# A graph attention layer on one core: edge values from four 64x64 products, weights in PSUM, clip on ScalarE, a new pace of the picks

## The chip, the core and the metric
One core of a Trainium2 chip. TensorE (PE; its weight loads are PEld) multiplies matrices into PSUM, VectorE (DVE) and ScalarE (ACT) work element by element on SBUF and PSUM, GpSimd (POOL) issues indirect DMAs, SyncE (SP) the plain ones. The metric is the time of one execution in microseconds on the device; lower is better.

## What is computed
6250 nodes with 64 features, 206250 edges sorted by destination, four heads of 16:

```python
score = (Kh[src] * Qh[dst] * (1.0 / np.sqrt(D)) * Ee).sum(-1)
score = jnp.exp(jnp.clip(score, -5.0, 5.0))
msg = Vh[src] * score[..., None]
wV = jax.ops.segment_sum(msg, dst, num_segments=n)
```
Kh, Qh and Vh are linear maps of the nodes' x, Ee is one of the edges' own 64 features (We, be). The output is layernorm(x + wV). All inputs are float32.

## The kernel before
Edges come in 1612 tiles of 128, in 202 groups of eight (g, the last one of four); two groups make a step s, except at the end. A first stage writes a table of K and V to memory and keeps a second form of x (parts, three bf16 parts) in SBUF. Then comes one loop over g, unrolled and written in the order in which each engine executes it: each engine works off its own instructions in that order, and waits for others by semaphores that the framework sets from the tiles that are read and written.

For each group:
- **K and V of the sources** (kv) come in two ways. Most tiles are fetched by one indirect DMA each, on POOL (gather_kv, L260), for a step four steps ahead. Two tiles in each of some groups are "picked" instead: DVE builds one-hot rows (hots, L644, pieces of up to five blocks, named hot), PE multiplies them with parts (picks, three products for each of 25 blocks of nodes), DVE selects the half (picked, L666), PE multiplies by the weights (picked_kv), ACT puts the result into kv (place_kv, L679). A batch is four tiles; 25 blocks are spread over three groups (9, 8 and 8) by first_unit, and 62 batches fit.
- **Edge values**: edges (L689) multiplies the block-diagonal 128x128 we_sb with the features of eight tiles, 128x512 in float32, into PSUM ee; two tiles lie above each other on the partitions. biased (L695, ACT) adds be and writes eb. It runs three groups ahead.
- **Queries**: queries multiplies one-hot rows (to, made on ACT at L243 and L249) with Q into qq, two halves of 64 partitions. terms (L708, DVE) multiplies eb by qq; turn (L713, PE) transposes the result into qe, one PSUM bank for even and one for odd g.
- **Scores**: products (L732 to L737, DVE) multiplies kv by qe, sums over each head and clips to -5 and 5; weigh (L741, ACT) is Exp; message (L753, DVE) multiplies V by the weights, both in SBUF, into qe.
- **Sum by destination**: keep (ACT, L765) and take (DVE, L770) split the message into three bf16 parts; sums (PE) multiplies them, once for each step, with one-hot columns of the destinations (of, L724, DVE) into pa, which shares a PSUM bank, room, with sum_. add (L805, L811, DVE) adds the three parts into sum_ and that into two rows of blocks, two groups after the step's end.

All products of the loop go through the helper product, so they have line 684; they are told apart by their tiles: pick, room (sums), ee, qq. Sums of a step are put between the picks of the next group, four after every two blocks, and the rest behind turn and queries. The add stands at the end of a group, except in the last steps.

PSUM is full: still (constants for the one-hots), room, two for picks, ee, qq, two of qe.

Of the kernel before, what the change touches and what calls it, by code (L numbers as in the profile page):

```python
# [1 line left out]

# [5 lines left out]
F32 = mybir.dt.float32  # L8
# [18 lines left out]
NS = len(STEPS)  # L27
NR2 = 112
ONES = NS - 8
# [18 lines left out]
TABLES = 4  # L48
BIG = N // P
REST = N - BIG * P  # L50


def tiles_of(g):
    return min(G, T - g * G)
# [6 lines left out]
def groups_of(s):  # L61
    return range(STEPS[s][0], STEPS[s][0] + STEPS[s][1])
# [5 lines left out]
UNITS = NB // 2  # L68
MOST = 5
LEAD = 6  # L70
# [2 lines left out]

def first_unit(g):

    return UNITS * ((g - LEAD) // 3) + (0, 9, 17)[(g - LEAD) % 3]


def when(k):
# [48 lines left out]
def tile_gnn(ctx: ExitStack, tc: tile.TileContext, x, x_blocks, by_rows, xT, wT, bias, beT, weT, eT, src, src_rows, dst,  # L128
             dst_rows, out):
    nc = tc.nc  # L130
    consts = ctx.enter_context(tc.tile_pool(name="consts", bufs=1))
# [28 lines left out]
    ident = consts.tile([P, P], F32, name="ident")  # L160
# [6 lines left out]
    row_b = consts.tile([P, 1], BF16, name="row_b")  # L167
    minus_row3 = consts.tile([P, 1], F32, name="minus_row3")
    one_p = consts.tile([P, 1], F32, name="one_p")
    ones_b = consts.tile([3, P], BF16, name="ones_b")  # L170
    key = consts.tile([P, T, 2], BF16, name="key")
    key_i = consts.tile([P, KEYS], I32, name="key_i")
# [6 lines left out]
    we_sb = consts.tile([P, 2 * C], F32, name="we_sb")  # L179
# [5 lines left out]
    be_col = consts.tile([P, 1], F32, name="be_col")  # L185
# [11 lines left out]
    ET, QW, at = {}, {}, {}  # L197
    SRC, FROM, ODD, KB, TO = ({} for _ in range(5))
# [89 lines left out]
    with tc.tile_pool(name="nodes", bufs=1) as nodes, \  # L288
# [27 lines left out]
        for i in range(NB // CB):  # L316
            s = slice(i * CB * P, (i + 1) * CB * P)
# [63 lines left out]
        def constants():  # L381
            nc.vector.tensor_scalar(from_row, row, -float(NB // 2), P + 0.75, op0=OP.mult, op1=OP.add)
            nc.vector.tensor_scalar(upper, row, C - 0.5, None, op0=OP.is_gt)
            nc.vector.tensor_copy(row_b, row_i)
            nc.vector.tensor_scalar(row_i, row_i, 1, None, op0=OP.arith_shift_right)
            nc.vector.tensor_scalar(half_b, row_i, P + 1.0, None, op0=OP.add)
            nc.vector.memset(one_p, 1.0)
            nc.vector.memset(ones_b, 1.0)

        def three_parts(out_, values, n, times):  # L390
# [206 lines left out]
    with tc.If(rv == 0) as branch:  # L597

        with tc.tile_pool(name="work", bufs=2) as work, \
                tc.tile_pool(name="accp", bufs=1) as accp, \  # L600
                tc.tile_pool(name="fixed", bufs=1, space=bass.MemoryType.PSUM) as fixed, \
                tc.tile_pool(name="psum", bufs=1, space=bass.MemoryType.PSUM) as psum:
            OH, OF, EB, TERM, MSG, SCORE, HOT = ({} for _ in range(7))
            still = fixed.tile([P, 4 * P], F32, name="still")
            col = still[:, :C].bitcast(BF16)
            block2 = still[:, C:C + NB].bitcast(BF16).rearrange("p (b c) -> p b c", c=2)
            nc.tensor.transpose(col, row_b[:, 0:1].to_broadcast([P, P]), ident_b)
            nc.tensor.transpose(still[:, C:C + NB].bitcast(BF16), half_b[:2 * NB].to_broadcast([2 * NB, P]),
                                ident_b[:2 * NB, :2 * NB])
            room = fixed.tile([P, 4 * P], F32, name="room")  # L610
            pa = room[:, :3 * C]
            sum_ = room[:, 3 * C:4 * C]
            px = [fixed.tile([P, 4 * P], F32, name=f"pick{k}") for k in range(2)]
            xs = [accp.tile([P, 4 * P], F32, name=f"x{k}") for k in range(2)]
            ee = fixed.tile([P, G // 2, P], F32, name="ee")
# [67 lines left out]
            def product(*aps, **kw):  # L683
                mark.append(nc.tensor.matmul(*aps, **kw))  # L684

            def edges(g):

                n = tiles_of(g) // 2
                product(ee[:, :n, :], we_sb, ET[g][:, :n, :], start=True, stop=True)  # L689

            def biased(g):

                n = tiles_of(g) // 2
                EB[g] = work.tile([P, G // 2, P], F32, name="eb")
                nc.scalar.activation(EB[g][:, :n], ee[:, :n], AF.Identity, bias=be_col)  # L695

            def queries(g):

                n = tiles_of(g)
                for u in range(2):  # L700
                    product(qq[u * C:(u + 1) * C, :n // 2, :], QW[g], TO[g][:, u:n:2, :],
                                     start=True, stop=True)

            def terms(g):
# [4 lines left out]

            def turn(g):  # L710

                for u in range(tiles_of(g) // 2):
                    nc.tensor.transpose(qe[g % 2][:, 2 * u:2 * u + 2, :].rearrange("p j c -> p (j c)"),  # L713
                                        TERM[g][:, u, :], ident)

            def onehot_edges(s):

# [11 lines left out]
            def products(g):  # L729
                n = tiles_of(g)  # L730
                prod = work.tile([P, G, C], F32, name="prod", bufs=1)
                nc.vector.tensor_mul(prod[:, :n, :], kv_of(g)[:, :n, :C], qe[g % 2][:, :n, :])  # L732
# [4 lines left out]
                nc.vector.tensor_scalar(score, score, -5.0, 5.0, op0=OP.max, op1=OP.min)  # L737

            def weigh(g):
                score = SCORE[g][:, :tiles_of(g)]  # L740
                nc.scalar.activation(score, score, AF.Exp)  # L741

            def message(g):
                s, k = place_of(g)
                n = tiles_of(g)
                if s < WHOLE:
                    if k == 0:
                        MSG[s] = work.tile([P, 2 * G, 3, C], BF16, name="msg")
                    to = qe[g % 2][:, :n, :]
                else:  # L750
                    MSG[s] = kvs[(s - 2) % KVB][:, G:, :C]
                    to = MSG[s][:, :n, :]
                nc.vector.tensor_mul(to.rearrange("p g (h d) -> p g h d", h=H),  # L753
                                     kv_of(g)[:, :n, C:].rearrange("p g (h d) -> p g h d", h=H),
                                     SCORE[g][:, :n, :, None].to_broadcast([P, n, H, D]))

            def part_of(g, i):

# [18 lines left out]

            def pa_of(s):

                return {NS - 3: px[0][:, :3 * C], NS - 2: px[1][:, :C], NS - 1: ee[:, 0, :C]}.get(s, pa)  # L780

            def sums(s, lo=0, hi=2 * G):
                n = tiles_in(s)
                for j in range(lo, min(hi, n)):
# [16 lines left out]
            def add(s):  # L801
                b = first_row(s) // P
                what = pa_of(s)
                if s < WHOLE:
                    nc.vector.tensor_reduce(sum_, what.rearrange("p (i c) -> p c i", i=3), axis=AX.X,  # L805
                                            op=OP.add)
                    what = sum_
                for k, mask in ((b, above), (b + 1, below)):
                    if 0 <= k < BIG + 1:
                        slot = slot_of(k)  # L810
                        nc.vector.scalar_tensor_tensor(slot, what, mask_of(mask, s), slot,  # L811
                                                       op0=OP.mult, op1=OP.add)
# [54 lines left out]
            for g in range(NG + 1):  # L867
# [36 lines left out]
                    hots(*mc)  # L904
                if parted:
                    take(g, 0)
                if g > groups_of(ONES - 1)[-1]:
                    for s in done:
                        add(s)
                if g - 1 in READY:  # L910
                    picked(READY.index(g - 1))
                if g - 2 in READY:
                    picked_kv(READY.index(g - 2))
                    place_kv(READY.index(g - 2))
                where.append(mark[-1])
# [231 lines left out]
```

## Time and profile before

| | us |
|---|---|
| median of 3 runs | 1745.33 (1743.85 to 1745.64) |
| the profiled execution | 1744.26 |
| its span, first to last instruction | 1742.4 |

The profile's page gives for each engine its busy time; groups of instructions by line with their tiles, count, busy time, mean duration in ns and the engine's idle time before them; the chain of waits, which goes back from the last instruction to whatever released it; and a timeline (start, duration, instruction). Each row of windows gives the length of a stretch and each engine's busy time in it. The time of one pass is read best as the distance between two starts, since matmuls are pipelined and a row's duration contains the pipeline's depth.

### The profile page before, as it was taken

Reading aid. Unit: us, or ns where it says so; the run is one execution under the profiler, and the core shown is the slowest. Engines: PE = TensorE matmul, PEld = TensorE weight load, DVE = VectorE, ACT = ScalarE, POOL = GpSimd, SP = SyncE. Lnnn points to the kernel's source line nnn. Section 1 sums busy time; section 2 is a strip of 40 time slices with the busy share of each in tenths; the row PEclk is TensorE's granted clock in tenths of the full one; section 3 lists DMA queues with packets and bytes.
Section 4 is the critical chain, followed back from the end, with each engine's and each line's share of the span. In section 5 each row is a group of like instructions: output and inputs, shape, how many; then the busy total and the mean of one; then the engine's idle time right before and its main releaser. Section 6 shows DMA issues by size and latency. Waiting matters only on the chain.

```text
span 1742.4 us, 26109 instructions
## 1 busy us (share of the span) xinstructions
PE 1661.7 (95%) x8456; PEld 881.2 (51%) x8611; DVE 1569.6 (90%) x2637; ACT 918.4 (53%) x1507; POOL 1310.5 (75%) x1374
## 2 busy tenths in 40 slices
PE   7779999999999999999999999999999999999964
PEld 6435555555555555555555555555555555555533
DVE  5689999999999999999999999999999999999976
ACT  3655555545555555555555555555555555555553
POOL 7777777777777777777777777777777777777775
PEclk9879999999999999999999999999999999999985
DMA  6744444343443443434434344344343443434331
GB/s 191 246 120 133 112 118 116 102 121 101 117 120 103 120 113 104 122 108 121 121 102 120 104 114 118 99 120 117 106 132 97 120 113 103 121 107 125 108 89 47
DMA packets 115144, 203.65 MB, mean 117 GB/s; under 512 B 55475, under 2 KB 56223, under 8 KB 114885
## 3 DMA queue, kind: packets, MB, share of 16 engines
q1 hardware_dynamic: 70914, 112.68, 21.7%
q0 software_dynamic: 43648, 88.17, 19.5%
q10 hardware_dynamic: 436, 1.04, 0.3%
q8 instruction: 69, 1.13, 0.3%
q14 instruction: 77, 0.63, 0.1%
HBM read 194.18 MB, written 7.59 MB: 116 GB/s over the span
## 4 chain that ended last, share of the span: by engine, by line
PE 90%; DMA 3%; DVE 2%; issue 2%; ACT 2%; POOL 1%; SPq 0%; POOLq 0%; DVEq 0%; ACTq 0%
PE pick L684 62%; PE ee L684 11%; PE room L684 7%; PE qe L713 5%; PE qq L684 4%; DMA kv<-kv_tab,src_i 2%; POOL kv L260 1%; PE ps L462 1%; DMA wkv<-in_wT 1%; DMA et<-in_eT 0%; PE pv L542 0%; DVE score L735 0%; DVE prod L732 0%; DVE term L708 0%; ACT eb L695 0%
## 5 line engine op out<-in xcount | busy, mean ns | idle before, releaser
L260 POOL DMA_INDIRECT kv<-kv_tab,src_i x1324 | 1270.7, 960 | 403.5 <-issue 197.1
L684 PE MATMUL pick<-hot,parts 128*128 128x512 bf16 x4495 | 1052.4, 379 | 8.3 <-issue 0.2
L684 PEld LDWEIGHTS <-parts 128*128 128x128 bf16 x4650 | 451.9, 98 | 527.1 <-issue 73.3
L644 DVE TENSOR_TENSOR hot<-from,still 128x2560 bf16<-128x2560 bf16 x366 | 460.0, 1257 | 0.0
L741 ACT ACTIVATE score<-score 128x32 f32<-128x32 f32 x202 | 46.3, 229 | 732.7 <-DVE score L737 732.7
L765 ACT ACTIVATE msg<-qe 128x512 bf16<-128x512 f32 x400 | 238.6, 596 | 35.8 <-DVE qe L753 26.9
L684 PE MATMUL ee<-et,we_sb 128*128 128x512 f32 x404 | 227.4, 645 | 7.1 <-ACT eb L695 6.1
L249 ACT ACTIVATE to<-to,one_p 126x1024 bf16<-126x1024 bf16 x198 | 226.5, 1144 | 0.0
L243 ACT ACTIVATE to<-kb,minus_row 126x1024 bf16<-126x1024 uint8 x198 | 224.6, 1134 | 0.0
L684 PE MATMUL room<-msg,of 128*128 128x192 bf16 x1592 | 200.2, 252 | 17.6 <-DVE y L811 11.3
L684 PEld LDWEIGHTS <-of 128*128 128x128 bf16 x1600 | 142.8, 100 | 109.5 <-DVE y L811 19.9
L770 DVE TENSOR_TENSOR msg<-qe,msg 128x512 bf16<-128x512 f32 x200 | 136.9, 685 | 67.4 <-ACT msg L765 61.3
L708 DVE TENSOR_TENSOR term<-eb,qq 128x512 f32<-128x512 f32 x202 | 137.0, 678 | 20.1 <-PE qq L684 15.8
L770 DVE TENSOR_TENSOR qe<-qe,msg 128x512 f32<-128x512 f32 x200 | 138.2, 691 | 18.2 <-ACT msg L765 18.2
L732 DVE TENSOR_TENSOR prod<-kv,qe 128x512 f32<-128x512 f32 x202 | 137.3, 680 | 8.2 <-DMA kv<-kv_tab,src_i 3.4
L735 DVE TENSOR_REDUCE score<-prod 128x32 f32<-128x512 f32 x202 | 138.3, 685 | 7.0
L713 PE MATMUL qe<-ident,term 128*128 128x128 f32 x806 | 126.2, 281 | 18.7 <-DVE term L708 18.7
L753 DVE TENSOR_TENSOR qe<-kv,score 128x512 f32<-128x512 f32 x200 | 139.0, 695 | 4.1 <-ACT score L741 4.1
L695 ACT ACTIVATE eb<-ee,be_col 128x512 f32<-128x512 f32 x202 | 135.1, 669 | 4.6 <-PE ee L684 4.6
L724 DVE TENSOR_TENSOR of<-still,key 128x2048 bf16<-128x2048 bf16 (+2 forms) x105 | 122.7, 1169 | 0.2
L713 PEld LDWEIGHTS qe<-ident,term 128*128 128x128 f32 x806 | 97.3, 144 | 49.8 <-DVE term L708 29.9
L684 PE MATMUL qq<-to,qw 126*64 126x512 bf16 x396 | 82.4, 413 | 0.0
(138 smaller groups left out, 855.5 us busy)
## 6 DMA issues: line engine op xcount, KB each, us to landing
et<-in_eT SPq DMA_DIRECT2D x100, 512.0 KB
kb<-key_tab SPq DMA_DIRECT2D x101, 252.0 KB
kv<-kv_tab,src_i POOLq DMA_INDIRECT x1324
srcs<-in_src_rows SPq DMA_DIRECT2D x62, 256.0 KB
qw<-q_tab SPq DMA_DIRECT2D x202, 15.8 KB
kv_tab<-kv_sb SPq DMA_DIRECT2D x4, 640.0 KB
q_tab<-q SPq DMA_DIRECT2D x5, 480.0 KB
y<-in_x_blocks SPq DMA_DIRECT2D x2, 512.0 KB
```

Of the source, the lines that this page charges most:

```text
L243: nc.scalar.activation(TO[g][:, :n, :], KB.pop(g)[:, :n * P].rearrange("p (j e) -> p j e", j=n), AF.Square, bias=minus_row3[:3 * W])
L249: nc.scalar.activation(TO[g][:, :n, :], TO[g][:, :n, :], AF.Relu, bias=one_p[:3 * W], scale=-1.0)
L260: return nc.gpsimd.indirect_dma_start(out=kv_of(g)[:, j, :], out_offset=None, in_=kv_tab[:, :], in_offset=bass.IndirectOffsetOnAxis(ap=src ...
L644: nc.vector.tensor_tensor(HOT[k][:, :hi - lo].rearrange("p b (a c) -> p b a c", c=2), pairs(FROM[m])[:, None].to_broadcast(shape), block2[ ...
L684: mark.append(nc.tensor.matmul(*aps, **kw))
L708: nc.vector.tensor_mul(TERM[g][:, :n], EB.pop(g)[:, :n], qq[:, :n])
L713: nc.tensor.transpose(qe[g % 2][:, 2 * u:2 * u + 2, :].rearrange("p j c -> p (j c)"), TERM[g][:, u, :], ident)
L732: nc.vector.tensor_mul(prod[:, :n, :], kv_of(g)[:, :n, :C], qe[g % 2][:, :n, :])
L735: nc.vector.tensor_reduce(score, prod[:, :n, :].rearrange("p g (h d) -> p g h d", h=H), axis=AX.X, op=OP.add)
L753: nc.vector.tensor_mul(to.rearrange("p g (h d) -> p g h d", h=H), kv_of(g)[:, :n, C:].rearrange("p g (h d) -> p g h d", h=H), SCORE[g][:, ...
L765: nc.scalar.activation(part, left, AF.Copy)
L770: nc.vector.tensor_sub(left if i == 0 else part_of(g, 2)[1], left, part)
```

## The change
- **Edge values** by four products for each group: weights and features are cut into two halves of 64 partitions (r), and each half into two halves of its tiles (u). Product (u, r) reads partitions of half r and writes partitions of half u. The two r go to two banks: room becomes two banks, and ee the first half of each. So tile k and tile k + 4 of a group now lie above each other, and queries, biased and turn follow.
- **Room**: pa and sum_ take the other half of the first bank; the other half of the second one holds three buffers of weights, and pa of the last step.
- **Weights** are written to PSUM by Exp. The clip leaves DVE: ACT makes Relu(5 - score), then Exp(5 - that), which is the exponential of the score's minimum with 5; the lower clip is the larger of the weight and exp(-5) inside the message's product, now a scalar_tensor_tensor.
- **Order**: sums stand behind queries as a whole; every add stands ahead of picked.
- **Picks**: 35 blocks in four groups instead of 25 in three. 65 batches fit, 12 more tiles are picked and as many fewer gathered.

```diff
-    return UNITS * ((g - LEAD) // 3) + (0, 9, 17)[(g - LEAD) % 3]
+    return (g - LEAD) * 35 // 4
...
-            room = fixed.tile([P, 4 * P], F32, name="room")
-            pa = room[:, :3 * C]
-            sum_ = room[:, 3 * C:4 * C]
+            room = fixed.tile([P, 2, 4 * P], F32, name="room")
+            ee = room[:, :, :2 * P].rearrange("p r (i e) -> p r i e", e=P)
+            pa = room[:, 0, 2 * P:2 * P + 3 * C]
+            sum_ = room[:, 0, 2 * P + 3 * C:2 * P + 4 * C]
+            weights = [room[:, 1, 2 * P + C + k * G * H:2 * P + C + (k + 1) * G * H]
+                       .rearrange("p (g h) -> p g h", g=G) for k in range(3)]
...
-                n = tiles_of(g) // 2
-                product(ee[:, :n, :], we_sb, ET[g][:, :n, :], start=True, stop=True)
+                n = tiles_of(g) // 4
+                for u in range(2):
+                    for r in range(2):
+                        rows = slice(r * C, (r + 1) * C)
+                        product(ee[u * C:(u + 1) * C, r, :n, :], we_sb[rows, rows],
+                                ET[g][rows, u * n:(u + 1) * n, :], start=True, stop=True)
...
-                nc.scalar.activation(EB[g][:, :n], ee[:, :n], AF.Identity, bias=be_col)
+                nc.scalar.activation(EB[g][:, :n].rearrange("p (i r) e -> p r i e", r=2),
+                                     ee[:, :, :n // 2], AF.Identity, bias=be_col)
...
-                nc.vector.tensor_scalar(score, score, -5.0, 5.0, op0=OP.max, op1=OP.min)
...
-                nc.scalar.activation(score, score, AF.Exp)
+                nc.scalar.activation(score, score, AF.Relu, bias=five_p, scale=-1.0)
+                WEIGHT[g] = weights[g % 3][:, :n]
+                nc.scalar.activation(WEIGHT[g], score, AF.Exp, bias=five_p, scale=-1.0)
...
-                nc.vector.tensor_mul(to.rearrange("p g (h d) -> p g h d", h=H),
-                                     kv_of(g)[:, :n, C:].rearrange("p g (h d) -> p g h d", h=H),
-                                     SCORE[g][:, :n, :, None].to_broadcast([P, n, H, D]))
+                nc.vector.scalar_tensor_tensor(
+                    to.rearrange("p g (h d) -> p g h d", h=H),
+                    WEIGHT.pop(g)[:, :, :, None].to_broadcast([P, n, H, D]), LEAST,
+                    kv_of(g)[:, :n, C:].rearrange("p g (h d) -> p g h d", h=H),
+                    op0=OP.max, op1=OP.mult)
...
-                if g > groups_of(ONES - 1)[-1]:
-                    for s in done:
-                        add(s)
+                for s in done:
+                    add(s)
...
-                summed = 0
-                for i, some in enumerate(by_two(todo)):
+                for some in by_two(todo):
                     picks(some)
-                    if i and parted and g - 1 in ends:
-                        sums(ends[g - 1], summed, summed + 4)
-                        summed += 4
...
-                    sums(ends[g - 1], summed)
+                    sums(ends[g - 1])
...
-                if g <= groups_of(ONES - 1)[-1]:
-                    for s in done:
-                        add(s)
```

More of the change, by code (lines that the diff above doesn't have):

```diff
@@ L1 @@
+import math
 from contextlib import ExitStack
@@ L50 @@
 REST = N - BIG * P
+CLIP = 5.0
+LEAST = math.exp(-CLIP)
 def tiles_of(g):
@@ L169, in tile_gnn @@
     one_p = consts.tile([P, 1], F32, name="one_p")
+    five_p = consts.tile([P, 1], F32, name="five_p")
     ones_b = consts.tile([3, P], BF16, name="ones_b")
@@ L387, in constants @@
             nc.vector.memset(one_p, 1.0)
+            nc.vector.memset(five_p, CLIP)
             nc.vector.memset(ones_b, 1.0)
@@ L602, in tile_gnn @@
                 tc.tile_pool(name="psum", bufs=1, space=bass.MemoryType.PSUM) as psum:
-            OH, OF, EB, TERM, MSG, SCORE, HOT = ({} for _ in range(7))
+            OH, OF, EB, TERM, MSG, SCORE, WEIGHT, HOT = ({} for _ in range(8))
             still = fixed.tile([P, 4 * P], F32, name="still")
@@ L700, in queries @@
                 for u in range(2):
-                    product(qq[u * C:(u + 1) * C, :n // 2, :], QW[g], TO[g][:, u:n:2, :],
+                    product(qq[u * C:(u + 1) * C, :n // 2, :], QW[g],
+                                     TO[g][:, u * n // 2:(u + 1) * n // 2, :],
                                      start=True, stop=True)
@@ L710, in turn @@
             def turn(g):
-                for u in range(tiles_of(g) // 2):
-                    nc.tensor.transpose(qe[g % 2][:, 2 * u:2 * u + 2, :].rearrange("p j c -> p (j c)"),
-                                        TERM[g][:, u, :], ident)
+                half = tiles_of(g) // 2
+                for k in range(half):
+                    nc.tensor.transpose(qe[g % 2][:, k:k + half + 1:half, :], TERM[g][:, k, :], ident)
             def onehot_edges(s):
@@ L736, in products @@
                                         axis=AX.X, op=OP.add)
-                nc.vector.tensor_scalar(score, score, -5.0, 5.0, op0=OP.max, op1=OP.min)
             def weigh(g):
-                score = SCORE[g][:, :tiles_of(g)]
-                nc.scalar.activation(score, score, AF.Exp)
+                n = tiles_of(g)
+                score = SCORE.pop(g)[:, :n]
+                nc.scalar.activation(score, score, AF.Relu, bias=five_p, scale=-1.0)
+                WEIGHT[g] = weights[g % 3][:, :n]
+                nc.scalar.activation(WEIGHT[g], score, AF.Exp, bias=five_p, scale=-1.0)
             def message(g):
@@ L778, in pa_of, with sums @@
             def pa_of(s):
-                return {NS - 3: px[0][:, :3 * C], NS - 2: px[1][:, :C], NS - 1: ee[:, 0, :C]}.get(s, pa)
-            def sums(s, lo=0, hi=2 * G):
+                return {NS - 3: px[0][:, :3 * C], NS - 2: px[1][:, :C], NS - 1: room[:, 1, 2 * P:2 * P + C]}.get(s, pa)
+            def sums(s):
                 n = tiles_in(s)
-                for j in range(lo, min(hi, n)):
+                for j in range(n):
                     product(pa_of(s), (OF if s >= WHOLE else OH)[s][:, j, :],
```

1 line of the change is left out of this document (removed).

## The prediction
> **What bounds the kernel now.** I read the page first, then windows of equal length, then the chain of waits inside two of them, then the gathers by themselves, and the last microseconds last.
>
> ```profile
> span 1742.4 us, 26109 instructions
> PE 1661.7 (95%) x8456; PEld 881.2 (51%) x8611; DVE 1569.6 (90%) x2637; ACT 918.4 (53%) x1507; POOL 1310.5 (75%) x1374
> ```
> ```profile
> 308.89:358.89 50.00, 49.74 (x260) 25.78 (x264) 46.54 (x74) 26.21 (x42) 37.81 (x41) 1.00 0.40 113
> 1008.85:1058.85 50.00, 49.74 (x260) 25.77 (x264) 45.92 (x73) 26.30 (x42) 37.81 (x41) 1.00 0.40 112
> ```
> The columns are length, PE, PEld, DVE, ACT, POOL. Six groups take 50.00 us, and PE is busy for 49.74 of them at full clock: PE sets the pace of the middle. DVE has some 4 us to spare, ACT half. POOL looks idle a quarter of the time, and that is the trap:
>
> ```profile
> L260 POOL DMA_INDIRECT kv<-kv_tab,src_i x1324: 940/944/1463, 55.6 to 1728.5; - x190
> ```
> ```profile
> L260 POOL DMA_INDIRECT kv<-kv_tab,src_i x1324 | 1270.7, 960 | 403.5 <-issue 197.1 <-PE pick L684 65.9 <-DMA kv<-kv_tab,src_i 48.8
> ```
> 1324 gathers start between 55.6 and 1728.5, one every 1672.9/1323 = 1.2645 us, and 403.5/1324 = 0.30 us of idle time before each is the same in every row that I looked at. So POOL runs without a pause, from the first gather to 14 us before the end (1742.4 - 1728.5). At the very end the consumer waits for it:
>
> ```profile
> 1728.53 3.02 DMA kv<-kv_tab,src_i
> 1731.67 0.43 DVE prod L732
> ```
> ```profile
> L732 DVE TENSOR_TENSOR prod<-kv,qe 128x512 f32<-128x512 f32 x202 | 137.3, 680 | 8.2 <-DMA kv<-kv_tab,src_i 3.4
> ```
> Over the whole run the consumer waits only 3.4 us for gathers. There are thus **two bounds that meet at the end**: PE's work per group, and POOL's count of gathers times their interval. To gain, both must fall.
>
> **POOL after.** Some gathers are longer than 0.94 us:
>
> ```profile
> 868.29 0.94 POOL L260 DMA_INDIRECT kv<-kv_tab,src_i  x1 [0.30 <-DVE score L737]
> 869.54 1.45 POOL L260 DMA_INDIRECT kv<-kv_tab,src_i  x1 [0.30 <-PE pick L684]
> 871.30 0.94 POOL L260 DMA_INDIRECT kv<-kv_tab,src_i  x1 [0.30 <-PE pick L684]
> ```
> ```profile
> 869.50 0.69 DVE L753 TENSOR_TENSOR qe<-kv,score 128x512 f32<-128x512 f32 x1
> ```
> The undisturbed interval is 869.54 - 868.29 = 1.25 us, the disturbed one 1.76. The long gather begins 0.04 us after the message product L753 and ends 0.80 us after that product does, as if it could not begin its own work before. L753 is the product whose two inputs, kv and score, both lie in SBUF. The change puts the weights into PSUM, so I expect the excess to go: 1324 x (1.2645 - 1.248), some 20 us. The pick rate removes 12 gathers (65 batches of four tiles instead of 62, worked out from first_unit and LAST). POOL would end at 55.6 + 1312 x 1.248 = 1693, and the kernel, 14 us later, at a **floor of 1707**. Without the first effect: 55.6 + 1312 x 1.2645 + 14 = 1729.
>
> **PE after, part by part.** The chain of waits in the steady stage, and single instructions there:
>
> ```profile
> 856.76 0.44 PE qe L713 x4
> 857.20 0.34 PE qq L684 x2
> 857.53 0.44 PE room L684 x4
> 857.97 0.89 PE ee L684 x2
> 858.86 5.18 PE pick L684 x24
> 864.04 0.44 PE qe L713 x4
> 864.48 0.34 PE qq L684 x2
> 864.81 1.05 PE ee L684 x2
> ...
> 868.46 0.33 PE room L684 x4
> ```
> ```profile
> 908.26 0.59 PE L684 MATMUL ee<-et,we_sb 128*128 128x512 f32 x1
> 908.69 0.38 PE L684 MATMUL pick<-hot,parts 128*128 128x512 bf16 x1
> ```
> - *Edge values.* One product is two passes (x2). It takes 0.89 us behind room, 1.05 behind qq (four of six groups): 1.0 in the mean. One pass over 512 columns takes 908.69 - 908.26 = 0.43, so over 256 columns 0.215. After the change eight such passes are issued per group, on four quarters of the array. If the four quarters work side by side, they take 2 x 0.215 = 0.43. No row shows four at once. The nearest is qq: its two halves, each 512 bf16 columns, take 0.34 together where one pick takes 5.18/24 = 0.216, so halves do run side by side; but the pair costs 0.12 more than one, and the room products behind it 0.11 more (0.44 against 0.33). I take 0.43 + 0.21 = **0.64 us** for the four, nearest to qq. The ends are 0.43 (nothing for entering and leaving the split array) and 8 x 0.215 + 0.23 = 1.95 (no overlap). Change: 202 x (0.64 - 1.0) = -73 us.
> - *Picks.* 65 x 25 - 62 x 25 = 75 blocks of three products: 225 x 0.216 = +48.6 us.
>
> ```profile
> L684 PE MATMUL pick<-w,x 128*128 128x128 f32 x496 | 71.8, 288 | 0.0
> L684 PE MATMUL pick<-bkv_p,ones_b 3*128 3x512 bf16 x62 | 23.8, 384 | 1.8 <-DVE x L666 1.8
> ```
> - Each batch also has its turn into kv: (71.8 + 23.8)/62 = 1.54 us, three more: +4.6.
> - *Sums* are the same 16 products in another place; turn and queries issue as many instructions as before. 0.
>
> PE in sum: -73 + 53 = **-20 us**, to 1722. That is above POOL's floor, so PE remains the bound and POOL keeps its lead until the end.
>
> **DVE, ACT and the new waits.**
>
> ```profile
> L644 DVE TENSOR_TENSOR hot<-from,still 128x2560 bf16<-128x2560 bf16 x183 | 270.7, 1479 | 0.0
> L644 DVE TENSOR_TENSOR hot<-from,still 128x2048 bf16<-128x2048 bf16 x61 | 73.9, 1212 | 0.0
> L753 DVE TENSOR_TENSOR qe<-kv,score 128x512 f32<-128x512 f32 x200 | 139.0, 695 | 4.1 <-ACT score L741 4.1
> L666 DVE SCALAR_TENSOR_TENSOR x<-odd,upper,pick 128x512 f32<-128x512 int32 x61 | 44.9, 736 | 0.0
> L737 DVE TENSOR_SCALAR score<-score 128x32 f32<-128x32 f32 x201 | 41.2, 205 | 7.0
> L770 DVE TENSOR_TENSOR msg<-qe,msg 128x512 bf16<-128x512 f32 x200 | 136.9, 685 | 67.4 <-ACT msg L765 61.3 <-ACT to L249 2.0
> ```
> - *One-hots for picks.* A block costs 1479 - 1212 = 267 ns, a piece 1479 - 5 x 267 = 144 besides. 75 blocks and 37 pieces more (372 to 409, since a piece may not cross a batch): 20 + 5.3 = +25 us. Three more x (736): +2.2.
> - *Message* becomes a scalar_tensor_tensor: 736 against 695, +8 us; no row shows it with a PSUM weight, I bound it by 0 and twice that. *Clip* goes: -41 us, or half if its drain was hidden already.
> - Sum between -6 and +15 us, under 0.5 us in a period. With 46 to 46.5 busy and 61.3/(202/6) = 1.8 of waits for ACT, DVE needs some 48.6 of a period that PE makes 49.4. Hidden, by little.
>
> ```profile
> 909.62 0.18 DVE L737 TENSOR_SCALAR score<-score 128x32 f32<-128x32 f32 x1
> 909.71 1.48 DVE L644 TENSOR_TENSOR hot<-from,still 128x2560 bf16<-128x2560 bf16 x1
> 909.83 0.23 ACT L741 ACTIVATE score<-score 128x32 f32<-128x32 f32 x1 [3.58 <-DVE score L737]
> 909.97 0.67 ACT L695 ACTIVATE eb<-ee,be_col 128x512 f32<-128x512 f32 x1
> 911.11 0.69 DVE L753 TENSOR_TENSOR qe<-kv,score 128x512 f32<-128x512 f32 x1
> ```
> - *Clip on ACT.* Relu is one more 0.23 between score and Exp, in place of 0.18 on DVE: the weights are there at about the same moment. Behind it on ACT wait eb, to and the copies of msg; ACT has half its time free.
> - *One bank for two things.* Weights and half of ee share a bank, pa and the other half another. The trace says what that means:
>
> ```profile
> PE room L684 <- DVE y L811: 11.3, 3, 4.7
> ```
> Sums wrote pa and waited for the reader of sum_, other columns of the same bank. So I take it that Exp now waits for ee of group g+3, and the message for eb. In the rows above eb ends at 910.64 and the message starts at 911.11; ee's last pass started at 908.26 and took 0.59, so 0.98 before Exp. The early sums cost the margin in every second group: up to 12 products more stand between qq and ee, 12 x 0.33/4 = 1.0 us. The cover is the hot piece of 1.48 us between score and message, which nearly always has five blocks (17 of 20 groups). Cost 0; if the cover is gone, 0.5 us in every second group.
> - The add's three instructions now come ahead of picked, the edges' one-hots and the second take on DVE. They are moved, not added, and behind them stands the wait for ACT's copy of msg (61.3 us in the row above) that they can fill: between -61 us and, with nothing absorbed, 3 x 0.354 x 102 = +108. I take 0: the number of instructions ahead of terms, the last of a group, is the same in both.
>
> ```profile
> L805 DVE TENSOR_REDUCE room<-room 128x64 f32<-128x192 f32 x102 | 36.1, 354 | 0.0
> ```
>
> **Rivals.**
> 1. *The passes queue.* Each product is two passes on the same quarter, issued one after the other; the second must wait for the first, and if the next product is not started past it, only neighbours overlap: pass 2 of one with pass 1 of the next. That is five slots, 5 x 0.215 = 1.08, with switching 1.31, against 1.0 now: +15 to +63 us, with the picks +68 to +116: **1812 to 1860**. It decides from the point where the four cost more than 1.0 - 53/202 = 0.74 us. For it: in the rows that I read PE starts in program order, and qq, which overlaps, has one pass for each half. Against: qq's halves start together, so a full half doesn't block its neighbour.
>    The Trainium skill, "TensorE: Matmul & The Clock Gate", Part 3, says that matmuls start and end strictly in program order, also on different tiles; by that rule it is this rival. The same section gives neighbours a start 4 ns apart, which the qq pair bears out (0.34 us for both).
> 2. *No overlap at all:* 1.95 us, +0.95 x 202 + 53: 1989. qq speaks against it.
> 3. *The bank waits decide:* 0.5 us in 101 groups, and DVE, with 0.7 us a period to spare, hands it to PE: 1725 + 50 = **1775**. Its point is where ee's end comes later than Relu's.
> 4. *The lock does not go:* POOL's floor is 1729 and becomes the bound, 1731 in all, 6 us above the forecast. The Trainium skill, "SBUF — State Buffer", Who interferes with whom, lets a VectorE instruction with two SBUF inputs block a GpSimd one that reads SBUF, and one with a single SBUF input not; by that rule the lock goes, and the long gather above agrees with its first half.
>
> **How the numbers follow.** The profiled execution took 1744.26 us, 1.9 above its span and 1.1 below the median of 1745.33. Forecast: 1722.9 + 1.9 = **1725**. Its own range: POOL's floor, 1707 + 2 = 1709, to ee at 0.80, 1757. Chances: forecast 0.60 (of which 0.04 within 0.2% and 0.04 above), rival 1 0.25, rival 2 0.05, rival 3 0.07, rival 4 0.03. A measurement of this kernel tells about 0.2%, 3.5 us, from no change. Faster: 0.52 + 0.03, and 0.02 for rival 3 at a small price: 0.57. Within 0.2%: 0.05. Slower: 0.38. For 8 in 10 the range takes the forecast's own, rival 3, rival 4 and the lower half of rival 1: 1709 to 1835.
>
> **What would show it.** In the chain of waits, ee at 0.6 to 0.7 us a group and pick at some 48 us more; PE still above 98% of a window of 50 us, and six groups in 49.4 of them. On POOL, 1312 gathers with a maximum near 0.95 us instead of 1.46, and an end with more than 3 us between last landing and use. ee at 1.1 or above means rival 1; DVE waiting ahead of the message for eb or Exp means rival 3. I would be wrong if PE had idle time while nothing else was full.

## The result, and the profile after

The changed kernel takes 1752.22 us (median of six runs, 1750.97 to 1753.05), the kernel before, run beside it, 1744.92 (1743.85 to 1746.65): a ratio of 1.0041, 95% interval 1.003 to 1.0053. The change costs 0.4%. The profiled execution took 1751.57.

The page's head for the kernel after:

```profile
span 1749.8 us, 29415 instructions
PE 1646.8 (94%) x9889; PEld 882.6 (50%) x10075; DVE 1573.9 (90%) x2479; ACT 1000.9 (57%) x1718; POOL 1281.6 (73%) x1362
```

PE's 1646.8 can't be set against before's 1661.7: both traces lack some records of PE (of after's 4875 products for picks 4689 are there, of before's 4650 it is 4495). So I go by times at which something starts. The first query product of group 21 and that of group 191 enclose 170 groups in which picks are made; what lies ahead of them and behind them I call the start and the end (picks are also made in 14 groups ahead of these and two behind). Windows cut at these two points, before first, then after (length, PE, PEld, DVE, ACT, POOL):

```profile
0.00:231.84 231.84, 197.10 (x858) 117.46 (x870) 183.19 (x366) 124.68 (x241) 173.74 (x190) 0.92 0.54 157
231.84:1647.64 1415.80, 1408.35 (x7334) 729.76 (x7475) 1317.73 (x2125) 752.61 (x1197) 1074.77 (x1120) 1.00 0.41 113
1647.64:1742.40 94.76, 56.22 (x268) 33.95 (x268) 68.69 (x148) 41.06 (x69) 62.02 (x66) 0.71 0.28 75
```
```profile
0.00:234.60 234.60, 189.84 (x1008) 115.36 (x1023) 183.50 (x351) 133.01 (x261) 174.75 (x193) 0.91 0.55 157
234.60:1653.80 1419.20, 1400.95 (x8568) 732.56 (x8737) 1326.29 (x1997) 821.20 (x1376) 1067.21 (x1128) 1.00 0.41 114
1653.80:1749.80 96.00, 55.99 (x318) 34.65 (x319) 64.14 (x132) 46.66 (x81) 39.62 (x42) 0.65 0.21 57
```

The first column is what counts: start +2.8, middle +3.4, end +1.2. Nowhere is there a gain, though the edge products took about the time that the forecast gave them. The chain of waits in the steady stage of after, and two places of PE's timeline:

```profile
867.22 0.44 PE qe L727 x4
867.65 0.34 PE qq L691 x2
867.99 0.59 PE room L691 x8
868.58 2.48 PE pick L691 x14
...
875.82 0.44 PE qe L727 x4
876.25 0.34 PE qq L691 x2
876.59 2.02 PE room L691 x24
```
```profile
901.92 0.66 PE L691 MATMUL room<-et,we_sb 64*64 64x256 f32 x8
902.52 0.82 PE L691 MATMUL pick<-hot,parts 128*128 128x512 bf16 x3
...
910.65 0.66 PE L691 MATMUL room<-et,we_sb 64*64 64x256 f32 x8
911.25 0.39 PE L691 MATMUL pick<-hot,parts 128*128 128x512 bf16 x1
```
"room" now holds the edge values too, so x8 are the eight passes of a group's four products, and x24 the same with the 16 sums ahead of them. The eight passes take 0.59 to 0.60 (902.52 - 901.92), where two passes over the whole array took 0.89 or 1.05. And the gathers of after by themselves:

```profile
L264 POOL DMA_INDIRECT kv<-kv_tab,src_i x1312: 939/944/1324, 55.5 to 1717.1; - x188
```

The last gather starts 11 us earlier than before's (1728.5), yet the kernel now runs on for 1749.8 - 1717.1 = 32.7 us behind it instead of 14. POOL no longer sets the end. Its own list of waits shows it:

```profile
POOL kv L264 <- issue: 197.8, 646, 0.6
POOL kv L264 <- PE pick L691: 83.2, 267, 1.1
...
POOL kv L264 <- PE qq L691: 34.6, 57, 8.0
```

The columns are total, count and longest. The 0.3 us before every gather is in these sums, whoever is named; before, no wait of a gather was longer than that. Now there are seven of 0.7 to 8.0 us, all from 1638 us on, and the trace names a product of PE for each. The program holds every gather of the loop until a product of PE that stands near it is done (behind, the same in both kernels): POOL has caught up with PE there, and waits for it. Of the 1312 gathers 20 take over 1000 ns, of before's 1324 it was 71.

So POOL has time over, and PE doesn't have less to do: the question is where the 20 us went that the forecast took off PE. The distance between the query products of two neighbouring groups gives a time for each group. I sorted the 170 groups by what PE has to do in them (number of pick products, a batch's turn or not, sums or not) and took the shortest of each kind as PE's own time. Eight groups of after are 0.5 to 1.2 us longer than the shortest of their kind; they make 7.1 of the 7.6 us by which the middle exceeds the sum of the shortest, 1411.6. In before that sum is 1415.6, and the middle is 0.2 above it. So **PE's own work in the middle fell by 4 us, not by 20**, and stalls of 7.4 took more than that away. In four of the eight the edge products wait for DVE's add, in one the sums wait for the message; the other waits are named for ACT's copy of msg, for picked, or for nothing. One of the four, PE first, then DVE:

```profile
666.24 0.41 PE L691 MATMUL qq<-to,qw 126*64 126x512 bf16 x2
667.61 0.66 PE L691 MATMUL room<-et,we_sb 64*64 64x256 f32 x8 [0.96 <-DVE y L828]
```
```profile
666.98 0.28 DVE L828 SCALAR_TENSOR_TENSOR y<-room,above,y 128x64 f32<-128x64 f32 x1
667.18 0.28 DVE L828 SCALAR_TENSOR_TENSOR y<-room,below,y 128x64 f32<-128x64 f32 x1
```

The edge products write ee, the add reads sum_, other columns of the same bank: ee starts 0.15 us after the add's last instruction ends (667.18 + 0.28). Before the change ee had a bank of its own, and no wait of ee for the add is in its list.

In the last groups, where there are no picks, another of these waits shows. ACT, then DVE, some 77 us from the end:

```profile
1672.51 0.32 ACT L754 ACTIVATE score<-score,five_p 128x32 f32<-128x32 f32 x1 [3.66 <-DVE score L748]
1672.86 0.29 ACT L756 ACTIVATE room<-score,five_p 128x32 f32<-128x32 f32 x1
1673.18 0.69 ACT L706 ACTIVATE eb<-room,be_col 128x512 f32<-128x512 f32 x1
```
```profile
1671.79 0.69 DVE L748 TENSOR_REDUCE score<-prod 128x32 f32<-128x512 f32 x1
1673.90 0.70 DVE L768 SCALAR_TENSOR_TENSOR qe<-room,kv 128x512 f32<-128x512 f32 x1 [1.43 <-ACT eb L706]
```

The timeline's last column is the idle time ahead of an instruction and what ended it. The weights are there at 1673.15, but the message starts at 1673.90, when eb has been read out of the same bank. In weights_alone_3 (below), where eb also comes behind Exp on ACT but ee has its own bank, the list of waits has none of the message for eb, only 13.0 us for its weights; pace25, with ee in the shared banks, has 24.9 us for eb. Between score and message DVE has nothing else here: no one-hots are built any more.

### The profile page after: what moved, and what is told of

It is laid out like the page before. It is cut to its first block, busy times and chain, and to the rows that moved or that the text cites. A ratio compares the mean times of both kernels' runs of the same rounds, so it can differ in the third digit from the quotient of the medians.

```text
span 1749.8 us, 29415 instructions
## 1 busy us (share of the span) xinstructions
PE 1646.8 (94%) x9889; PEld 882.6 (50%) x10075; DVE 1573.9 (90%) x2479; ACT 1000.9 (57%) x1718; POOL 1281.6 (73%) x1362
## 4 chain that ended last, share of the span: by engine, by line
PE 75%; DVE 12%; ACT 7%; issue 3%; DMA 3%; POOL 1%; DVEq 0%; POOLq 0%; SPq 0%; ACTq 0%
PE pick L691 55%; PE room L691 12%; PE qe L727 4%; PE qq L691 3%; DVE score L748 2%; ACT eb L706 2%; DVE prod L745 1%; DVE term L721 1%; DMA kv<-kv_tab,src_i 1%; DVE hot L651 1%; ACT to L247 1%; ACT msg L782 1%; DVE qe L787 1%; DVE qe L768 1%; PE ps L467 1%
## 5 line engine op out<-in xcount | busy, mean ns | idle before, releaser
L264 POOL DMA_INDIRECT kv<-kv_tab,src_i x1312 | 1241.7, 946 | 421.2 <-issue 197.8
L691 PE MATMUL pick<-hot,parts 128*128 128x512 bf16 x4689 | 1064.2, 380 | 13.1 <-issue 4.9
L691 PEld LDWEIGHTS <-parts 128*128 128x128 bf16 x4875 | 467.4, 98 | 580.6 <-issue 49.2
L651 DVE TENSOR_TENSOR hot<-from,still 128x2560 bf16<-128x2560 bf16 (+4 forms) x403 | 481.7, 1203 | 0.0
L754 ACT ACTIVATE score<-score,five_p 128x32 f32<-128x32 f32 x202 | 64.9, 321 | 674.6 <-DVE score L748 672.0
L691 PE MATMUL room<-msg,of 128*128 128x192 bf16 x1592 | 156.5, 254 | 30.4 <-DVE y L828 13.6
L768 DVE SCALAR_TENSOR_TENSOR qe<-room,kv 128x512 f32<-128x512 f32 x200 | 139.9, 700 | 45.9 <-ACT eb L706 39.2
L691 PEld LDWEIGHTS <-of 128*128 128x128 bf16 x1600 | 133.3, 101 | 56.1 <-issue 31.7
L691 PE MATMUL room<-et,we_sb 64*64 64x256 f32 (+1 forms) x1616 | 137.9, 412 | 21.8 <-ACT msg L782 6.0
L787 DVE TENSOR_TENSOR qe<-qe,msg 128x512 f32<-128x512 f32 x200 | 138.9, 695 | 12.5 <-ACT msg L782 12.5
L706 ACT ACTIVATE eb<-room,be_col 128x512 f32<-128x512 f32 x202 | 138.6, 686 | 9.0 <-PE room L691 2.5
```

The costliest lines, as they stand in the source:

```text
L264: return nc.gpsimd.indirect_dma_start(out=kv_of(g)[:, j, :], out_offset=None, in_=kv_tab[:, :], in_offset=bass.IndirectOffsetOnAxis(ap=src ...
L651: nc.vector.tensor_tensor(HOT[k][:, :hi - lo].rearrange("p b (a c) -> p b a c", c=2), pairs(FROM[m])[:, None].to_broadcast(shape), block2[ ...
L706: nc.scalar.activation(EB[g][:, :n].rearrange("p (i r) e -> p r i e", r=2), ee[:, :, :n // 2], AF.Identity, bias=be_col)
L768: nc.vector.scalar_tensor_tensor(to.rearrange("p g (h d) -> p g h d", h=H), WEIGHT.pop(g)[:, :, :, None].to_broadcast([P, n, H, D]), LEAST ...
L787: nc.vector.tensor_sub(left if i == 0 else part_of(g, 2)[1], left, part)
```

## The experiments

The theory: the change pays for its edge products with picks that it needn't have made. PE and POOL are two bounds that meet at the end; the quicker gathers, no longer held up by the message, lower POOL's, the edge products PE's, and the 12 tiles more for PE take the second away again. Then the old pace of 25 blocks in three groups, with the rest of the change, should be near the forecast. The rival: the new waits (bank, DVE) hold the kernel up, whatever the picks; then the pace is worth little, and an order with fewer such waits much.

**The old pace alone put back** (pace25) and **eb ahead of the scores on ACT** (ebfirst), alone and together; and, in the kernel before, **the new pace alone** (picks_alone):

```diff
-    return (g - LEAD) * 35 // 4
+    return UNITS * ((g - LEAD) // 3) + (0, 9, 17)[(g - LEAD) % 3]
```
```diff
+                if g + 3 < NG:
+                    biased(g + 3)
                 if now:
...
-                if g + 3 < NG:
-                    biased(g + 3)
```

> The changed kernel with the picks back at 25 blocks in three groups; nothing else undone. Theory, picks: PE sets the pace, and the added picks (some 46 us of products and 5 of batch turns) ate what the edge products gave back (some 55). Without them PE's own sum falls by about 51, and POOL becomes the bound: 1324 gathers at 1.249 us from 55.5 end at 1709, and the span some 14 to 16 us later, 1723 to 1726 (1725 to 1728 in all). Rival, chain: the new waits for a shared bank (Exp behind ee, message behind eb, ee behind add) set the pace; then the picks are not what costs, and it stays at 1745 or above.

> The changed kernel at 35 blocks in four groups with ACT's eb of group g+3 ahead of Relu and Exp of group g, so that the message needn't wait for eb behind Exp. Theory, picks: the middle is PE's and stays; only the groups without picks at both ends gain, where the message waited 1.43 us for eb (12.5 us in the last 110, 8.2 in the first 240, not all of it on the path): 1738 to 1746. Rival, chain: the middle gains too, below 1736.

> Both: picks at 25 in three, and eb ahead of Relu and Exp. Theory, picks: POOL is the bound throughout, so the ends gain little beside pace25: 1719 to 1728. Rival, chain: it differs from ebfirst by less than 5 us.

> The kernel before with the new pace of the picks alone: 35 blocks in four groups. Theory, picks: PE was full, so all of the added work shows: some 46 us of products and 5 to 6 of batch turns, 1790 to 1800. Rival, chain: if PE's picks could hide in waits, under 1775.

Measured beside a kernel before of 1744.67 (median of ten): pace25 1728.36 (1727.59 to 1731.09), ratio 0.9907 [0.989, 0.9924]. ebfirst 1738.56 (1736.2 to 1740.26), 0.9964 [0.9953, 0.9975]. Both together 1727.3 (1726.66 to 1728.38), 0.9901 [0.9885, 0.9918]. picks_alone 1795.06 in one run. pace25 ends 0.4 us above the theory's range, the other three inside it. But the middle of ebfirst gains too, which only the rival had: theory and rival both hold a part, 24 us and 13.7 us of 1752, and they don't add up: with both edits 25. Windows of ebfirst at the same two points:

```profile
233.83:1646.13 1412.30, 1411.85 (x8738) 732.36 (x8737) 1314.03 (x1997) 836.39 (x1376) 1068.71 (x1128) 1.00 0.41 114
1646.13:1737.10 90.97, 53.45 (x320) 32.85 (x319) 64.14 (x132) 46.77 (x81) 42.54 (x45) 0.67 0.23 63
```

With eb read earlier PE is busy for 1411.85 of 1412.30 in the middle: the stalls are gone, and 1412 is what PE itself needs with the change's picks, 3.5 less than before's 1415.8. The middle gains 6.9, the end 5.0, the start 0.8. The message no longer waits for eb. Its waits in the whole run, after first, then ebfirst, where it waits for its own weights:

```profile
DVE qe L768 <- ACT eb L706: 39.2, 42, 2.7
```
```profile
DVE qe L768 <- ACT room L756: 16.2, 17, 2.9
```

picks_alone gives the price of the picks where nothing else changes. Its middle, and its products:

```profile
233.59:1700.79 1467.20, 1466.98 (x7716) 754.64 (x7715) 1343.90 (x2163) 756.24 (x1206) 1095.43 (x1130) 1.00 0.40 110
```
```profile
L684 PE MATMUL pick<-hot,parts x4875: 379/379/380, 114.2 to 1716.1; 128*128 128x512 bf16 x195
```

1467.2 - 1415.8 = +51.4 us in the middle, PE busy throughout, for the 71 of the 75 blocks that lie in it. Over the 185 groups from the query products of group 8 to those of group 193, which hold nearly all picks, it is 1594.5 - 1539.5 = +55.0: 75 blocks and three turns cost about what the forecast said (53). It is one run.

pace25's middle and its end:

```profile
233.69:1623.89 1390.20, 1368.18 (x8496) 710.18 (x8495) 1300.56 (x1957) 814.76 (x1367) 1052.01 (x1110) 1.00 0.42 115
1623.89:1729.30 105.41, 56.98 (x323) 34.94 (x322) 65.81 (x133) 46.66 (x81) 69.32 (x74) 0.64 0.27 72
```
```profile
L264 POOL DMA_INDIRECT kv<-kv_tab,src_i x1324: 939/946/1322, 55.6 to 1714.5; - x190
```

The middle falls by 25.6 against before, and PE is idle in it for 22 us; the end grows by 10.6. The last gather starts 14.8 us before the end, as in before: POOL is the bound again, at 1324 x 1.254 us. ebfirst on top of it brings 1 us more, hardly beyond the spread of the runs: POOL's last gather comes only 3 us earlier (1711.5 in ebfirst_pace25).

**Each half of the change at the old pace.** quads_alone_3 keeps the four products and the order, and puts clip, weights and message back as they were; weights_alone_3 keeps weights in PSUM, the clip on ACT and the order, and puts one 128x512 edge product back into a bank of its own, with the old order of the tiles. From the two edits:

```diff
+                nc.vector.tensor_scalar(score, score, -5.0, 5.0, op0=OP.max, op1=OP.min)
...
-                nc.scalar.activation(score, score, AF.Relu, bias=five_p, scale=-1.0)
-                WEIGHT[g] = weights[g % 3][:, :n]
-                nc.scalar.activation(WEIGHT[g], score, AF.Exp, bias=five_p, scale=-1.0)
+                nc.scalar.activation(score, score, AF.Exp)
+                WEIGHT[g] = score
```
```diff
-            room = fixed.tile([P, 2, 4 * P], F32, name="room")
-            ee = room[:, :, :2 * P].rearrange("p r (i e) -> p r i e", e=P)
...
+            room = fixed.tile([P, 4 * P], F32, name="room")
+            ee = fixed.tile([P, G // 2, P], F32, name="ee")
...
-                for u in range(2):
-                    for r in range(2):
-                        rows = slice(r * C, (r + 1) * C)
-                        product(ee[u * C:(u + 1) * C, r, :n, :], we_sb[rows, rows],
-                                ET[g][rows, u * n:(u + 1) * n, :], start=True, stop=True)
+                product(ee[:, :n, :], we_sb, ET[g][:, :n, :], start=True, stop=True)
```

> Four edge products at 25 blocks in three groups, clip on DVE, weights in SBUF, once more beside a kernel before at its usual time. Theory, two bounds: POOL keeps its long gathers and is the bound, 1738 to 1746. Rival: PE alone set the time, 1690 to 1710; or the moved clip made pace25's gain, 1728.

> One edge product, weights in PSUM, clip on ACT, 25 in three, once more. Theory, two bounds: the long gathers go, PE is as full as before: 1738 to 1746. Rival: the lock was the bound, 1725 to 1730.

quads_alone_3 took 1741.3 (1738.78 to 1743.79), ratio 0.9978 [0.9969, 0.9988]; weights_alone_3 1743.53 (1741.39 to 1745.41), 0.999 [0.998, 0.9999]; before 1745.22. Gathers, first of quads_alone_3, then of weights_alone_3:

```profile
L264 POOL DMA_INDIRECT kv<-kv_tab,src_i x1324: 940/945/1467, 55.7 to 1724.8; - x190
```
```profile
L264 POOL DMA_INDIRECT kv<-kv_tab,src_i x1324: 940/944/1321, 55.5 to 1710.8; - x190
```

With the weights in SBUF the long gathers are back (maximum 1467; 70 over 1000 ns), the last one starts at 1724.8, and the end comes 14.7 us later: POOL's bound. With the weights in PSUM (13 over 1000 ns) POOL is done at 1710.8, but the kernel only 31.6 later: PE's bound, with a middle of 1414.1. Each half moves one bound and leaves the other. At the old pace the halves are worth 4 and 2 us, both together 16 (1744.67 - 1728.36).

**Paces in between**, with eb ahead: 42 blocks in five groups and 60 in seven (`(g - LEAD) * 42 // 5`, `* 60 // 7`), 63 and 64 batches.

> eb ahead of Relu and Exp at 42 blocks in five groups, 1320 gathers, another attempt beside a kernel before at its usual time. Theory, two bounds: POOL sets the time, 1720 to 1725. Rival, DVE is the bound: 1727 and above.

> The same at 60 blocks in seven groups, 1316 gathers, another attempt. Theory, two bounds: 1717 to 1724. Rival, DVE is the bound: 1727 and above.

1723.32 (1722.99 to 1723.72), 0.9878 [0.9862, 0.9895], and 1720.44 (1719.67 to 1722.37), **0.9863 [0.9847, 0.988]**. Both lie in the range of the two bounds and below 1727, where DVE as the bound would have left them. The second is the fastest kernel of this study, 1.4% below the one before. Its gathers and its windows:

```profile
L264 POOL DMA_INDIRECT kv<-kv_tab,src_i x1316: 938/944/1318, 55.4 to 1700.6; - x188
```
```profile
232.31:1626.41 1394.10, 1390.84 (x8634) 722.22 (x8633) 1301.45 (x1989) 834.18 (x1373) 1054.27 (x1116) 1.00 0.41 115
1626.41:1719.40 92.99, 57.08 (x344) 34.74 (x343) 66.82 (x135) 47.09 (x81) 56.86 (x61) 0.70 0.26 72
```

PE is full in the middle (1390.84 of 1394.1), and POOL ends 18.8 us before the end, hardly more than the 14 to 15 that the kernel needs behind the last gather when it waits for it. That is the balance: four picked tiles cost PE some 18 us (55.0/3) and spare POOL 5 (4 x 1.25). Between 25/3 and 35/4 the two bounds cross, and of the paces tried 60/7 lies nearest to the crossing.

**The same kernels at another speed: inconclusive.** The two halves and the two paces were first run where the kernel before, too, took 1.17 to 1.19 times as long (2050 to 2075 us). The record has them on chips 1, 0 and 11, the other runs on chips 10, 0 and 9, so that the chip's number alone does not tell the two apart.

> The changed kernel at 25 blocks in three groups with the clip back on DVE and the weights back in SBUF; the four edge products and the order of sums and add stay. Theory, two bounds: PE is relieved by some 50 us, but POOL keeps its long gathers (a mean of about 1.26 us) and is the bound: 1324 of them end near 1725, and the time is 1738 to 1746, no gain. Rival: if the gathers only looked like a bound and PE alone set the time, 1690 to 1710; if what pace25 gained came from the moved clip, about as pace25, 1728.

> The changed kernel at 25 blocks in three groups with one edge product of 128 x 512 in a bank of its own; weights in PSUM, clip on ACT and the new order stay. Theory, two bounds: the long gathers go (maximum near 1.0 us in place of 1.46), POOL could end 18 us earlier, but PE is as full as before: 1738 to 1746. Rival: if the lock was the bound, 1725 to 1730.

> Four edge products, weights in PSUM, eb ahead of Relu and Exp, and 42 blocks in five groups (63 batches, 1320 gathers). Theory, two bounds: PE has room at this pace (0.245 us a group less than at 35 in four), POOL sets the time and loses four gathers, 5 us: 1720 to 1725. Rival, DVE is the bound: as ebfirst_pace25 or slower, 1727 and above.

> The same with 60 blocks in seven groups (64 batches, 1316 gathers). Theory, two bounds: POOL's floor falls by another 5 us, to 1717, and PE's sum, 0.117 us a group under that at 35 in four, comes to about the same: 1717 to 1724. Rival, DVE is the bound: 1727 and above.

Ratios there, two for each half and three for each pace: quads_alone 1.0071 and 1.0085, weights_alone 1.0012 and 1.0017, ebfirst_pace42 1.0089, 1.0089 and 1.0098, ebfirst_pace60 1.0055, 1.0056 and 1.0061, each to about 0.002. They agree with each other and contradict the runs above. In their traces single instructions last as long as elsewhere, but there is idle time between them on every engine for which the profile shows no releaser. PE's weight loads of quads_alone there, and of pace25 at the usual speed (quads_alone_3, the same kernel as quads_alone, has 146.9 us in 528 waits):

```profile
PEld L691 <- issue: 370.9, 892, 4.0
```
```profile
PEld L691 <- issue: 151.2, 518, 2.4
```

What causes it stays open, and so does why the kernels with four products lose more there than weights_alone: they have some 2300 instructions more (28688 against 26366), but no run shows that this is the reason, and there is no profile of the kernel before at that speed. Every other number in this document is from runs beside which the kernel before takes 1744 to 1745.

## Why the prediction was wrong, step by step

Forecast 1725 with a span of 1722.9, measured 1752 with 1749.8: 27 us more, and on the other side of 1745, inside the range.

- **Four products in 0.64 us instead of 1.0: right for the four, a little high for the one.** From the last product ahead to the first one behind, over the 170 groups, the four take 0.595 behind queries and 0.69 behind sums, 0.643 in the mean. ee before took 0.89 behind sums, and behind queries 0.96, or 1.06 where a batch's turn came next: 0.97 in the mean, where the chain of waits shows 1.05 for all behind queries.
- **Rivals 1 and 2, passes that queue: wrong.** Matmuls on room that start between 910.64 and 910.70 us:

```profile
L691 PE MATMUL room<-et,we_sb x4: 427/427/427, 910.6 to 910.7; 64*64 64x256 f32 x4
```

  The four first passes start within 0.02 us of each other (by their records at 910.650, .656, .663 and .670), the four second ones 0.27 us later. So a product's second pass does not hold the next product's first one back. The rule of the Trainium skill that I weighed ("TensorE: Matmul & The Clock Gate", Part 3, order of starts and ends) would give rival 1 only if both passes of a product stand ahead of the next product's. The trace has neighbours start 6 to 7 ns apart, a little more than the 4 ns there, and does not show how the passes are ordered in the program.
- **"PE in sum: -73 + 53 = -20": this is the step that failed.** The picks were nearly right (+55 against +53). The gain of the edge products was too large, in two ways. First, the gain of one group: pace25 has all of the change but its picks, and sorted as above, the 185 groups that hold its picks come to 1481.9 us of PE's own time, against 1539.3 before: -57.4, or 0.31 a group instead of 0.36. The rows above give 0.33 for the products alone; no run separates the rest, the new place of the sums, put at 0, among it. Second, I multiplied by all 202 groups. PE sets the pace only where there are picks; in the other 17 groups, 8 at the start and 9 at the end, it waits, so that a shorter product ends nothing sooner there, and 6 us of the sum were not to be had. Windows of before: the first 8 groups, the 13 with picks ahead of the middle, and the last 9 with all that follows:

```profile
72.81:124.83 52.02, 35.80 (x141) 17.28 (x141) 37.81 (x61) 28.31 (x44) 39.53 (x42) 0.74 0.52 147
124.83:231.84 107.01, 106.43 (x552) 54.83 (x562) 100.79 (x161) 58.19 (x93) 81.11 (x86) 1.00 0.42 116
1664.35:1742.40 78.05, 39.56 (x180) 25.25 (x179) 55.24 (x125) 32.70 (x55) 49.27 (x53) 0.65 0.26 69
```

  In after the 185 groups come to 1535.1 of PE's own time, 4.2 less than before, and the 170 of the middle to 4.0 less. The share of 95% for the whole span hid the groups in which PE waits, and my windows were from the middle alone.
- **"One bank for two things. Cost 0": the second step that failed.** ebfirst takes 12.7 us off the span with nothing but an earlier read of the bank. The cover that I named, the hot piece between score and message, is missing in the end, where I had not looked, and does not always hold in the middle: of the 39.2 us that the message waits for eb, 12.5 lie behind 1640 us and 18.5 between 240 and 1640. There PE, which sets the pace, hides most of it. What costs is that DVE comes late: in four of the eight groups above PE then waits for its add, which uses the bank that PE is to write, and in a fifth for its message. With eb read earlier nearly all of the stalls are gone (0.8 us of 7.6 left). Rival 3 was the right mechanism at a quarter of its 50 us (12.7), and in part in other places. The Relu and the Exp cost 0.32 and 0.29 in the rows above, not 0.23 each. And the sum for DVE, -6 to +15, leaves out the bounds that it names for the message, 0 and twice 8: with them it is -14 to +23.
- **The lock goes: right**, and with it rival 4 is refuted. The gathers over 1000 ns fell from 71 to 20; at the old pace there are 70 with the weights back in SBUF, and 13 with them in PSUM and one edge product (25 in pace25, with four). The forecast read this from one gather; all of them say the same. Before, 83 gathers start while the message still has over 0.1 us to run, and 63 of these are long. Of 678 that start so beside the one-hots for picks, terms, prod or take, the same kind of instruction (TENSOR_TENSOR) with one input in PSUM, none is. After, 90 start beside the message, and none is long. So it is the place of the weights. The 20 that are left start beside other instructions, nine of them beside one that the rows above don't show (odd, L234). "SBUF — State Buffer", Who interferes with whom, in the Trainium skill agrees for these instructions: two inputs in SBUF block a GpSimd instruction that reads SBUF, one doesn't. POOL's floor was put at 1693 for the last gather; it came at 1717.1, 20 us later than without the seven waits for PE, which a bound doesn't have.
- **"To gain, both must fall": right, and not followed to its end.** With 1707 for POOL and 1722 for PE my own numbers said that fewer picks would be better. The change's 12 tiles bought POOL time that it could not use.

These make up the 27 us: 15.5 from the sum of PE (-19.5 forecast, -4.0 in the middle), 7.4 from the stalls in the middle, and 4.0 by which start and end grew. The end's part is the bank wait, as far as ebfirst gets 5.0 back there. Of the 15.5 the smaller gain of a group is about 9 and the 17 groups are 6. The start's 2.8 stays open: the starts of the ten kernels run at this speed lie between 230.0 and 234.6 us, and picks_alone, which changes nothing else, has 233.6 where before has 231.8.

What pace25 waits for in its middle is open too. PE has 22 us to spare there; DVE, with its waits for ACT, needs 8.1 us a group by the prediction's count, and 1390.2/170 = 8.18; but POOL, without a pause, gives the same time. The paces in between speak for POOL: they give DVE and PE more to do and POOL fewer gathers, and are faster than ebfirst_pace25. Which of the two each of PE's pauses waits for is not shown.

## What to carry to other kernels

When two engines bound a kernel, count each one's gain only over the stretch in which it sets the pace, and let a knob that moves work between them be set last: here four picked tiles added 18 us to one engine and took 5 off the other, and the best pace lay between the old and the new one. Here a PSUM bank shared by two tenants brought new waits between their readers and writers; look for such waits where the usual cover is missing (the last groups, the steps with an extra instruction), and try first to mend them by the order on the reading engine's queue.

## What the hardware showed that I had not expected

- Four float32 products of 64x64 by 256 columns run side by side on the array: eight passes in 0.60 us, where two passes of 128x128 by 512 columns took 0.89 to 1.06, depending on the products around them. Behind sums the eight passes take 0.1 us more than behind queries, which are split too.
- On 128x32 elements an Exp with no bias tile took 0.23 us, a Relu with one 0.32, and an Exp with one and its output in PSUM 0.29.
- An indirect DMA beside a TENSOR_TENSOR with both inputs in SBUF took up to 1.46 us instead of 0.94 (63 of 83); beside one with an input in PSUM it never took over 0.97 (678 of them).
- POOL shown as busy for 75% can be full: in pace25, whose end waits for it, gathers start every 1.254 us, 0.95 of them busy and 0.30 idle.
